# A graph layer's prologue done block by block: norm, projection and the first attention of a block in turn

## The chip, the cores and the metric

One core of one Trainium2 chip. The metric is the device time of one execution in microseconds (us). The kernel uses five engines that run side by side, each with its own instruction queue: TensorE (PE; its weight loads are listed as PEld), VectorE (DVE), ScalarE (ACT), GpSimd (POOL), and SyncE (SP), which here only issues DMAs. Matrix operands are 32-bit floats throughout.

## The reference

One layer of a graph transformer over 3125 nodes with 256 features and 100,000 edges. Its three branches are:

```python
xn = layernorm(x)                                           # no gain, no bias
# 1. graph branch
m   = relu(concat([xn[src], edge_attr], 1) @ W1.T + b1)     # 100000 x 256
h_N = segment_sum(m, dst)                                   # dst is sorted
g   = relu(concat([xn, h_N], 1) @ W2.T);  g = g / max(norm(g), 1e-12)
# 2. mixer: 4 layers of linear attention and a feed-forward part on xn
for i in range(4):
    h = layernorm(xm) * ln1_g[i] + ln1_b[i]
    q = softmax(heads(h @ Wq[i]) * s, over features)
    k = softmax(heads(h @ Wk[i]) * s, over nodes);  v = heads(h @ Wv[i])
    xm = xm + (q @ (k.T @ v)) @ Wo[i] + bo[i]
    h = layernorm(xm) * ln2_g[i] + ln2_b[i]
    xm = xm + gelu(h @ W1[i] + b1[i]) @ W2[i] + b2[i]
x = x + g + xm
# 3. mixture of experts: 16 experts, 2 for each node, then a layernorm
x = x + layernorm(y + moe(y)) * gamma + beta,  with y = layernorm(x)
```

The first step of mixer layer 0 is a layernorm of `xn`, which is itself a layernorm of `x`.

## The kernel before

The nodes lie in 25 tiles of 125 rows, grouped in seven blocks of 4, 4, 4, 4, 4, 3 and 2 tiles (`BLOCKS`). All 25 tiles stay on the chip in `xm`, which holds first `x`, then `xn`, then the mixer's running sum.

The prologue has four parts, written out one after the other. First, SP issues the loads: all of `x` in block order, then `w1h` (the node part of the graph branch's W1), `w1w` (its edge part), the bias `b1`, the edge indices `src_i` and `dst_i`, the norm gains `lnp`, and Wk, Wq, Wv of layer 0. Second, the destinations of the edges are turned into windows: `dst_i` is cast to `drel`, the least destination of each strip of edges is found (`least`, `lcol`, transposes `least_ps`, `base_ps` and `most_ps` on PE), and it is subtracted. Third, for each block: statistics (lines 90 and 91), a reciprocal root (`rsqrt`, lines 108 to 114, eleven small operations that depend on each other), a normalisation on DVE (line 122), transposes into `xnT` (line 144, copied out by ACT on line 244), and the projection `proj = xn @ w1h` (line 251), to which DVE adds `b1` (line 254) before it is stored to memory. Fourth, the attention of layer 0 is done block by block: statistics once more, a second `rsqrt` and normalisation into `xh1`, transposes `hT_ps` (stage_t1), k with a running maximum over nodes (stage_k), q (stage_q), transposes of exp(k) and q (stage_ek, stage_qT), and the sum over nodes `m_ps` (stage_m). When all blocks are summed, `context(l)` makes from it the matrix `mo` (first PE step `meanT_ps`), and the feed-forward part of layer 0 starts.

The edge work of the graph branch has no stage of its own. Edges come in 784 chunks of 128; eight chunks make one of 98 groups. `load_chunk` gathers the rows of `proj` for a chunk with an indirect DMA from POOL (line 273); `message_step` multiplies the edge features (`pw`, line 312), adds them to the gathered rows on DVE (line 316) and takes relu on ACT (line 317); `sum_step` sums a group into its windows on PE (`pq`, line 297), transposes (`win_ps`, line 288) and adds to `hNT` on DVE (line 291). A gather can start when all of `proj` is stored. These steps are dealt out between the mixer's matmuls: every stage calls `worked(columns)` with the columns that PE has just been given, the variable `place` advances by `columns * (98 + 1 + 1.25) / total`, and what is due by then is issued. `total` is the number of columns in four attentions and three feed-forward parts, so the edge work is spread from the first attention block to the end of mixer layer 2. Before a gather, POOL makes a one-element copy (`tick`, line 349) of something the stage has just written, so that gathers do not run ahead.

PE, ACT and POOL run in the order in which the program is written (`manual_schedule`); the order on DVE and SP is chosen by the framework's scheduler when the kernel is built.

Of the kernel before, what the change touches and what calls it, by code (L numbers as in the profile page):

```python
# [8 lines left out]
F32 = mybir.dt.float32  # L9
# [55 lines left out]
def gps_layer(ctx: ExitStack, tc: tile.TileContext, a, out):  # L65
# [60 lines left out]
    with ExitStack() as ph:  # L126
# [49 lines left out]
        b1 = tmp.tile([P, D], F32, tag="b2", name="b1")  # L176
# [6 lines left out]
        for r in BLOCKS:  # L183
            by_parts(nc.sync, xm[:, r[0]:r[-1] + 1, :], xv[:, r[0]:r[-1] + 1, :])
        nc.sync.dma_start(w1h, a["gnn_W1h"].rearrange("(c p) n -> p c n", p=P))
        for s in range(S):
            nc.sync.dma_start(w1w[s * W:s * W + 3, :], a["gnn_W1w"])
        nc.sync.dma_start(b1, rows_bcast(a["gnn_b1"], P))
        nc.sync.dma_start(src_i, a["src_c"])
        nc.sync.dma_start(dst_i, a["dst_c"])  # L190
        nc.sync.dma_start(lnp, a["mix_ln"])
        nc.sync.dma_start(ffb, a["mix_b1"])
        wt = {}

        def load(l, *names):
            for k in names:
# [4 lines left out]
        load(0, "Wk", "Wq", "Wv")  # L201


        nc.gpsimd.iota(slot, pattern=[[1, W]], base=0, channel_multiplier=0,
                       allow_small_or_imprecise_dtypes=True)
        nc.vector.tensor_copy(drel, dst_i)
        strips = drel.rearrange("p (g j) -> p g j", j=SC)
        least = edge.tile([P, NS], F32, name="least", bufs=1)
        nc.vector.tensor_reduce(least, strips, axis=AX.X, op=ALU.min)
        lcol = edge.tile([P, 1], F32, name="lcol", bufs=1)  # L210
        for s0 in range(0, NS, NG):
            part = least[:, s0:s0 + NG]
            ps = mm_tile("least_ps")[:NG, :P]
            nc.tensor.transpose(ps, part, ident)
            nc.vector.tensor_reduce(lcol[:NG], ps, axis=AX.X, op=ALU.min)
            ps = mm_tile("base_ps")[:, :NG]
            nc.tensor.transpose(ps, lcol[:NG].to_broadcast([NG, P]), ident[:NG, :NG])
            nc.vector.tensor_copy(part, ps)
        nc.vector.tensor_copy(base_i, least[:1, :])
        nc.vector.tensor_tensor(strips, strips, least[:, :, None].to_broadcast([P, NS, SC]),  # L220
                                op=ALU.subtract)

        for p0, p1 in ((NE % P, 2 * (NE % P)), (2 * (NE % P), P)):
            nc.vector.memset(drel[p0:p1, NCH - 1:NCH], -1.0)
        nc.vector.memset(drel[:, NCH:], -1.0)
        most = edge.tile([P, 1], F32, name="most", bufs=1)
        nc.vector.tensor_reduce(most, drel, axis=AX.X, op=ALU.max)
        ps = mm_tile("most_ps")[:1, :P]
        nc.tensor.transpose(ps, most, ident)
        nc.vector.tensor_reduce(most[:1], ps, axis=AX.X, op=ALU.max)  # L230
        nc.vector.tensor_scalar(far_i, most[:1], float(W), None, op0=ALU.is_ge)


        for r in BLOCKS:
            for t in r:
                stats(tmp, xm[:, t, :], t)
            finish_stats(r)
            for t in r:
                normalize(xm[:, t, :], xm[:, t, :], t)
            xnT = tmp.tile([P, KC, BT * TP], F32, tag="hT", name="xnT", bufs=2)  # L240
            for q in groups(len(r), 2):
                t0, n, o = r[q[0]], len(q), q[0] * TP
                ps = transposed(xm[:, t0:t0 + n, :], n, "xnT_ps")
                nc.scalar.copy(xnT[:, :, o:o + n * TP], ps)
            nc.sync.dma_start(xnT_d[:, :, cols(r[0], len(r))], xnT[:, :, :len(r) * TP])
            for q in groups(len(r), 2):
                t0, n, o = r[q[0]], len(q), q[0]
                pp = mm_tile("proj_ps")[:TP].rearrange("p (i d) -> p i d", d=D)
                for i in range(n):
                    for c in range(KC):  # L250
                        nc.tensor.matmul(pp[:, i, :], xnT[:, c, cols(o + i)], w1h[:, c, :],
                                         start=(c == 0), stop=(c == KC - 1))
                pj = tmp.tile([TP, 2, D], F32, tag="pj", name="pj", bufs=2)
                nc.vector.tensor_add(pj[:, :n, :], pp[:, :n, :],
                                     b1[:TP, None, :].to_broadcast([TP, n, D]))
                by_parts(nc.sync, by_tile(proj)[:, t0:t0 + n, :], pj[:, :n, :])
# [4 lines left out]
        def load_chunk(c):  # L261

            g, j = divmod(c, G)
            if j == 0:
                ea = edge.tile([P, SC * P], F32, name="ea")
                for s in range(S):
                    e0 = (g * S + s) * SC * P
                    nc.sync.dma_start(ea[s * W:s * W + 3, :], a["eaT"][:, e0:e0 + SC * P])
                groups_[g] = [], ea
            gats = groups_[g][0]  # L270
            if j % (G // 2) == 0:
                gats.append(edge.tile([P, 2, SC, D], F32, name="gat", bufs=6))
            nc.gpsimd.indirect_dma_start(  # L273
                out=gats[-1][:, (j // SC) % 2, j % SC, :], out_offset=None, in_=proj,
                in_offset=bass.IndirectOffsetOnAxis(ap=src_i[:, c:c + 1], axis=0))
# [26 lines left out]
        def message_step(g):  # L302
# [7 lines left out]
            for i in range(SC):  # L310
                for s in range(S):
                    nc.tensor.matmul(pws[s][:, i, :], ea[s * W:s * W + 3, i * P:(i + 1) * P],  # L312
                                     w1w[s * W:s * W + 3, :], start=True, stop=True)
# [23 lines left out]
        total = DEPTH * attention + (DEPTH - 1) * (forward + 60 * D)  # L337
        place = -LEAD
        tick = tmp.tile([1, 1], F32, name="tick")

        def worked(columns, mark=None):


            nonlocal place
            place += columns * (NG + 1 + LEAD) / total
# [17 lines left out]
        st = {}  # L363

# [249 lines left out]
        with tc.manual_schedule(engines=in_order):  # L614

            for b in range(NB + 1):
                if b < NB:
                    stage_stats(b)
                    stage_ln1(b)
                    stage_t1(0, b)  # L620
                if b > 0:
                    stage_ek(0, b - 1)
                    stage_qT(0, b - 1)
                if b < NB:
                    stage_k(0, b)
                    stage_q(0, b)
                if b > 0:
                    stage_m(0, b - 1)
            for l in range(last):
# [47 lines left out]
        def any_order():  # L677
# [13 lines left out]
            def chunk(e0, n):  # L691
# [15 lines left out]
                nc.sync.dma_start(ea[:3, :n], a["eaT"][:, ds])  # L707
# [17 lines left out]
                nc.tensor.matmul(pw[:n, 0, :], ea[:3, :n], w1w[:3], start=True, stop=True)  # L725
# [427 lines left out]
def device_arrays(inputs):  # L1153
# [14 lines left out]
    d = {"x": i["x"], "eaT": np.pad(i["edge_attr_3"].T, ((0, 0), (0, fill))), "src": i["src"], "dst": i["dst"]}  # L1168
    d["src_c"], d["dst_c"] = chunked(i["src"]), chunked(i["dst"])
    w1 = i["L0_gnn_W1"]  # L1170
    d["gnn_W1h"], d["gnn_W1w"] = w1[:, :D].T, w1[:, D:].T
    d["gnn_b1"] = i["L0_gnn_b1"]
# [33 lines left out]
```

## Time and profile before

| what | us |
|---|---|
| median of 3 runs (2003.48 to 2004.11) | 2003.74 |
| profiled execution, its own time | 1999.63 |
| its span, first to last instruction | 1997.9 |
| PE busy in the span | 1800.4 (90%) |
| DVE busy | 1188.0 (59%) |
| POOL busy | 1135.1 (57%) |
| ACT busy | 726.0 (36%) |
| mean granted TensorE clock | 0.958 of full |

The profiled execution is one run; its own time is 1.7 us over its span and 4.1 us (0.2%) under the median of the timed runs. The page divides the span into 40 slices of about 50 us. A group row gives line, engine, operation, names and shapes, count, then busy time and mean duration of one in ns, and after the second bar the idle time of that engine just before these instructions, with what ended it. A wait row names who waited for whom, the total in us, how often, and the longest. In the windows table each row is a stretch of the span, with the busy time of each engine in it. In the timeline, each row has a start, a length, the engine and line, what it writes and reads, and the idle time ahead of it in brackets.

### The profile page before, as it was taken

The numbers are of one execution on the slowest core, as the hardware profiler recorded it, in microseconds if no ns is written. First come the engines' busy times: TensorE is split into PE (matmuls) and PEld (weight loads), VectorE is DVE, ScalarE is ACT, GpSimd is POOL, SyncE is SP. The second block draws the span as 40 slices with busy tenths as digits, with TensorE's granted clock in tenths as the row PEclk, the third lists the DMA queues.
The fourth block names the chain that finished last, engine by engine and source line by source line (L and its number), as shares of the span: only waits on it lengthen the run. The fifth ranks groups of instructions, "written<-read, shape, count | busy, mean of one in ns | idle before, by whom it ended". The sixth has DMA issues, their size and how long they took to land. (4 is left out here: it accounts for less than half of the span.)

```text
span 1997.9 us, 30925 instructions
## 1 busy us (share of the span) xinstructions
PE 1800.4 (90%) x9749; PEld 1263.7 (63%) x9749; DVE 1188.0 (59%) x3910; ACT 726.0 (36%) x1305; POOL 1135.1 (57%) x1469
## 2 busy tenths in 40 slices
PE   2888899999988999999889999998999994999963
PEld 2656466666664666666646666676777783788841
DVE  8677546766666466767565667665555653333326
ACT  0344334434443444445433444453222221222212
POOL 1366766667666776767667776772213445555512
PEclk9998899999998999999989999998999996999977
DMA  6422322223243322323433222233211103777744
GB/s 186 139 78 84 103 77 76 83 75 89 83 134 89 91 83 76 89 78 92 128 94 90 79 86 78 86 86 114 66 32 27 30 19 97 251 260 261 267 131 127
DMA packets 83416, 210.46 MB, mean 105 GB/s; under 512 B 26287, under 2 KB 41927, under 8 KB 78510
## 3 DMA queue, kind: packets, MB, share of 16 engines
q0 software_dynamic: 44800, 118.16, 20.2%
q1 hardware_dynamic: 37368, 87.03, 13.8%
q10 hardware_dynamic: 1078, 3.20, 0.6%
q8 instruction: 83, 1.36, 0.3%
q14 instruction: 87, 0.71, 0.1%
HBM read 187.06 MB, written 21.19 MB: 104 GB/s over the span
## 5 line engine op out<-in xcount | busy, mean ns | idle before, releaser
L273 POOL DMA_INDIRECT gat<-proj,src_i x784 | 761.1, 971 | 219.1 <-issue 162.8
L542 PE MATMUL f_ps<-h2T,ww 128*128 128x500 f32 (+2 forms) x896 | 360.9, 551 | 8.3 <-ACT h2T L354 6.3
L317 ACT ACTIVATE gat<-gat 128x512 f32<-128x512 f32 x392 | 237.5, 630 | 343.3 <-DVE gat L316 322.6
L552 PE MATMUL f_ps<-ww,gT 128*125 128x256 f32 x1600 | 360.3, 381 | 0.0
L316 DVE TENSOR_TENSOR gat<-gat,pw 128x512 f32<-128x512 f32 x392 | 245.5, 680 | 154.6 <-PE pw L312 138.0
L552 PEld LDWEIGHTS f_ps<-ww,gT 128*125 128x125 f32 x1600 | 295.0, 188 | 55.5 <-issue 11.4
L542 PEld LDWEIGHTS f_ps<-h2T,ww 128*128 128x128 f32 x896 | 166.0, 192 | 172.6 <-issue 120.5
L544 ACT ACTIVATE gT<-f_ps,ffb 128x500 f32<-128x500 f32 (+2 forms) x224 | 135.4, 631 | 134.4 <-PE f_ps L542 133.7
L297 PE MATMUL pq<-gat,hot 128*32 128x256 f32 x1568 | 131.4, 402 | 11.2 <-ACT gat L317 10.8
L291 DVE TENSOR_TENSOR hNT<-hNT,win_ps 128x64 f32 x392 | 84.7, 216 | 69.1 <-PE win_ps L288 57.0
L866 POOL DMA_INDIRECT slots<-rec,at x50 | 59.5, 1189 | 110.3 <-DVE rs_u L113 64.1
L312 PE MATMUL pw<-w1w,ea 3*128 3x256 f32 x1568 | 116.2, 406 | 1.6 <-ACT ekT L408 1.6
L557 DVE TENSOR_TENSOR xm<-xm,f_ps 125x512 f32<-125x512 f32 (+1 forms) x52 | 34.7, 667 | 136.7 <-PE f_ps L552 133.9
L1061 PE MATMUL e_ps<-ew,hs 128*128 128x256 f32 x464 | 112.8, 381 | 2.2 <-DVE o L1065 2.2
L1068 POOL DMA_INDIRECT outs<-o,ids x58 | 57.4, 989 | 99.5 <-DVE o L1066 94.9
L508 PE MATMUL y_ps<-mo,qT 128*125 128x256 f32 x400 | 96.2, 391 | 6.7 <-DVE mo L499 6.7
L90 DVE BATCH_NORM_STATS2 bnst<-xm 125x6 f32<-125x256 f32 x250 | 97.9, 416 | 5.5 <-DMA xm<-x 3.4
L312 PEld LDWEIGHTS pw<-w1w,ea 3*128 3x128 f32 x1568 | 72.9, 187 | 44.1 <-issue 34.4
L456 PE MATMUL m_ps<-xh,ek 125*128 125x257 f32 x400 | 97.8, 397 | 1.3 <-ACT ek L442 1.3
L1061 PEld LDWEIGHTS e_ps<-ew,hs 128*128 128x128 f32 x464 | 85.2, 190 | 20.4 <-issue 4.5
L419 PE MATMUL q_ps<-wwq,hT 128*125 128x256 f32 x400 | 94.9, 387 | 3.6 <-DVE gat L316 2.4
L524 POOL TENSOR_TENSOR xm<-xm,b 125x1024 f32<-125x1024 f32 (+2 forms) x28 | 59.9, 2139 | 66.4 <-DVE xh L122 50.1
(210 smaller groups left out, 2631.7 us busy)
## 6 DMA issues: line engine op xcount, KB each, us to landing
ew<-ffn_w SPq DMA_DIRECT2D x37, 1154.0 KB
gat<-proj,src_i POOLq DMA_INDIRECT x784
ww<-mix_W SPq DMA_DIRECT2D x8, 1024.0 KB
ea<-eaT SPq DMA_DIRECT2D x392, 3.0 KB
proj<-pj SPq DMA_DIRECT2D x12, 224.0 KB
ogs<-outs SPq DMA_DIRECT2D x6, 448.0 KB
ogs<-outs ACTq DMA_DIRECT2D x6, 448.0 KB
out<-ogs SPq DMA_DIRECT2D x6, 448.0 KB
```

What stands on the lines that cost most here:

```text
L90: nc.vector.bn_stats(st, src)
L273: nc.gpsimd.indirect_dma_start(out=gats[-1][:, (j // SC) % 2, j % SC, :], out_offset=None, in_=proj, in_offset=bass.IndirectOffsetOnAxis(a ...
L297: nc.tensor.matmul(pq[s * W:(s + 1) * W, :], hot[:, s * SC + i, :], gats[s // 2][:, s % 2, i, :], start=(i == 0), stop=(i == SC - 1))
L312: nc.tensor.matmul(pws[s][:, i, :], ea[s * W:s * W + 3, i * P:(i + 1) * P], w1w[s * W:s * W + 3, :], start=True, stop=True)
L316: nc.vector.tensor_add(msg, msg, pws[s])
L317: nc.scalar.activation(msg, msg, AF.Relu)
L456: nc.tensor.matmul(ps, st["ek", b][:, i, c * P:(c + 1) * P], xh1s[b % 2][:, i, :], start=(i == 0), stop=(i == n - 1))
L508: nc.tensor.matmul(ps[:, i, :], qT[:, c, cols(t0 + i)], mo[:, c, :], start=(c == 0), stop=(c == KC - 1))
L542: nc.tensor.matmul(ps, wt["W1"][:, c, f * P:(f + 1) * P], st["h2T", b][:, c, :m], start=(c == 0), stop=(c == KC - 1))
L544: nc.scalar.activation(gT[:, f, :m], ps, AF.Gelu, bias=ffb[:, l, f:f + 1])
L552: nc.tensor.matmul(ps[:, i, :], st["gT", b][:, f, cols(o + i)], wt["W2"][:, f, :], start=(f == 0), stop=(f == NF - 1))
L1061: nc.tensor.matmul(ps[:, j, :], x["hs"][:, f, j * P:(j + 1) * P], x["w2"][:, f, :], start=(f == 0), stop=(f == NEF - 1))
```

## The change

The prologue's four parts become one loop over blocks. For a block, the norm, the projection and the attention follow each other, and the next block's norm and projection are written between the attention's stages of this one.

- The loads are put in the order of use: the first four tiles of `x` in two pairs, `w1h`, `lnp`, then the other blocks, with Wk and Wq after block 1 and `dst_i` after block 3; the rest comes last.
- The second layernorm's statistics are not taken. With v the variance of a row of `x` and e the small constant, a row of `xn` has mean 0 and variance v/(v+e), so the two norms follow from v: `stage_xn` computes v+e and (e(v+e)+v)(v+e), takes the reciprocal roots of both at once (`rs`, 8 columns for a block), normalises `xm` with the first, and multiplies to get the factor from `xn` to `xh1`. `stage_xh1` applies that factor on ACT.
- The bias `b1` becomes a fourth edge feature with value 1, so `eaT` and `w1w` have four rows in place of three, and the projection is copied out by ACT with no bias added. It is stored a block at a time. `xnT` and the projection are staged in the memory of `gT` and `xh`.
- The window computation becomes a generator, `windows()`, whose PE steps are issued one by one between the stages of blocks 2 to 5.
- `worked` does nothing until block 5 is through (`spread`), and `total` counts three attentions in place of four. So the edge work starts behind the sixth of seven blocks.

```diff
-        for r in BLOCKS:
-            by_parts(nc.sync, xm[:, r[0]:r[-1] + 1, :], xv[:, r[0]:r[-1] + 1, :])
-        nc.sync.dma_start(w1h, a["gnn_W1h"].rearrange("(c p) n -> p c n", p=P))
...
-        load(0, "Wk", "Wq", "Wv")
+        for r in (range(0, 2), range(2, 4)):
+            by_parts(nc.sync, xm[:, r[0]:r[-1] + 1, :], xv[:, r[0]:r[-1] + 1, :])
+        nc.sync.dma_start(w1h, a["gnn_W1h"].rearrange("(c p) n -> p c n", p=P))
+        nc.sync.dma_start(lnp, a["mix_ln"])
+        for i, r in enumerate(BLOCKS[1:]):
+            by_parts(nc.sync, xm[:, r[0]:r[-1] + 1, :], xv[:, r[0]:r[-1] + 1, :])
+            if i == 0:
+                load(0, "Wk", "Wq")
+            if i == 2:
+                nc.sync.dma_start(dst_i, a["dst_c"])
...
+        load(0, "Wv")
+        def windows():
...
+                yield
+                ps = mm_tile("least_ps")[:NG, :P]
+                nc.tensor.transpose(ps, part, ident)
...
-                pj = tmp.tile([TP, 2, D], F32, tag="pj", name="pj", bufs=2)
-                nc.vector.tensor_add(pj[:, :n, :], pp[:, :n, :],
-                                     b1[:TP, None, :].to_broadcast([TP, n, D]))
-                by_parts(nc.sync, by_tile(proj)[:, t0:t0 + n, :], pj[:, :n, :])
...
-                    nc.tensor.matmul(pws[s][:, i, :], ea[s * W:s * W + 3, i * P:(i + 1) * P],
-                                     w1w[s * W:s * W + 3, :], start=True, stop=True)
+                    nc.tensor.matmul(pws[s][:, i, :], ea[s * W:s * W + 4, i * P:(i + 1) * P],
+                                     w1w[s * W:s * W + 4, :], start=True, stop=True)
...
-        total = DEPTH * attention + (DEPTH - 1) * (forward + 60 * D)
+        total = (DEPTH - 1) * (attention + forward + 60 * D)
         place = -LEAD
+        spread = False
...
+            if not spread:
+                return
...
+        def stage_xn(b):
+            r = BLOCKS[b]
+            n = len(r)
+            for t in r:
+                stats(tmp, xm[:, t, :], t)
+            rs = tmp.tile([TP, 3, 2, BT], F32, name="rs", bufs=3)
...
+            nc.vector.tensor_scalar(rs[:, 0, 0, :n], v, EPS, None, op0=ALU.add)
+            nc.vector.scalar_tensor_tensor(rs[:, 0, 1, :n], rs[:, 0, 0, :n], EPS, v, op0=ALU.mult, op1=ALU.add)
+            nc.vector.tensor_mul(rs[:, 0, 1, :n], rs[:, 0, 1, :n], rs[:, 0, 0, :n])
+            rsqrt(rs[:, 1], rs[:, 0], rs[:, 2])
+            for i, t in enumerate(r):
+                nc.vector.tensor_scalar(xm[:, t, :], xm[:, t, :], mv[:, t, 0:1], rs[:, 1, 0, i:i + 1],
+                                        op0=ALU.subtract, op1=ALU.mult)
+            nc.vector.tensor_mul(rs[:, 2, 0, :], rs[:, 0, 0, :], rs[:, 1, 1, :])
+        def stage_xh1(b):
+            for i, t in enumerate(BLOCKS[b]):
+                nc.scalar.activation(xh1s[b % 2][:, i, :D], xm[:, t, :], AF.Copy,
+                                     scale=st["rs", b][:, 2, 0, i:i + 1])
+        def stage_xnT(b):
...
+                ps = transposed(xm[:, t0:t0 + n, :], n, "xnT_ps")
+                nc.scalar.copy(xnT[:, :, cols(o, n)], ps)
+            nc.sync.dma_start(xnT_d[:, :, cols(r[0], len(r))], xnT[:, :, :len(r) * TP])
+        def stage_proj(b):
...
+                        nc.tensor.matmul(pp[:, i, :], st["xnT", b][:, c, cols(o + i)], w1h[:, c, :],
+                                         start=(c == 0), stop=(c == KC - 1))
+                nc.scalar.copy(pj[:, o:o + n, :], pp[:, :n, :])
+            by_parts(nc.sync, by_tile(proj)[:, r[0]:r[-1] + 1, :], pj[:, :len(r), :])
...
+            prepared = windows()
+            stage_xn(0)
+            stage_xh1(0)
+            stage_xnT(0)
+            stage_proj(0)
+            stage_xn(1)
+            stage_t1(0, 0)
             for b in range(NB + 1):
                 if b < NB:
-                    stage_stats(b)
-                    stage_ln1(b)
-                    stage_t1(0, b)
-                if b > 0:
-                    stage_ek(0, b - 1)
-                    stage_qT(0, b - 1)
-                if b < NB:
                     stage_k(0, b)
+                    if b + 2 < NB:
+                        stage_xn(b + 2)
                     stage_q(0, b)
+                if b > 1:
+                    next(prepared, None)
                 if b > 0:
                     stage_m(0, b - 1)
+                if b + 1 < NB:
+                    stage_xh1(b + 1)
+                    stage_xnT(b + 1)
+                    if b > 1:
+                        next(prepared, None)
+                    stage_proj(b + 1)
+                    stage_t1(0, b + 1)
+                if b < NB:
+                    if b > 1:
+                        next(prepared, None)
+                    stage_ek(0, b)
+                    stage_qT(0, b)
+                if b == NB - 2:
+                    for _ in prepared:
+                        pass
+                    spread = True
```

## The prediction

> **What bounds the kernel now.** I read the page first, then the start of the span in the windows table, then PE's waits, the timeline of PE, and POOL's groups.
>
> ```profile
> span 1997.9 us, 30925 instructions
> PE 1800.4 (90%) x9749; PEld 1263.7 (63%) x9749; DVE 1188.0 (59%) x3910; ACT 726.0 (36%) x1305; POOL 1135.1 (57%) x1469
> ...
> 0.00:38.00 38.00, 2.92 (x9) 1.29 (x10) 32.88 (x192) 1.28 (x1) 6.12 (x8) 1.00 0.70 194
> 38.00:70.80 32.80, 30.50 (x151) 25.50 (x151) 24.31 (x127) 6.79 (x13) 0.00 (x0) 1.00 0.53 179
> 70.80:200.50 129.70, 110.85 (x677) 78.82 (x676) 89.87 (x233) 57.03 (x112) 79.39 (x122) 0.95 0.30 85
> 200.50:240.00 39.50, 32.08 (x170) 18.04 (x171) 23.41 (x82) 12.96 (x22) 27.88 (x34) 0.83 0.35 103
> 240.00:600.00 360.00, 347.98 (x2023) 234.47 (x2021) 227.48 (x671) 159.10 (x282) 247.59 (x352) 0.98 0.30 88
> ```
>
> PE bounds the middle (348 of 360 us busy from 240 to 600), so time is to be had where PE idles. In the first 38 us PE works 2.9 us; DVE is busy for 32.9.
>
> ```profile
> PE least_ps L214 <- DVE rs_u L113: 30.4, 1, 30.4
> ```
>
> PE's queue begins with the window transposes, whose input DVE makes after most of its norms: 30.4 us in one wait, the largest of PE.
>
> ```profile
> 38.02 1.87 PE L144 MATMUL xnT_ps<-ident,xm 125*128 125x125 f32 x8
> 39.73 4.76 PE L251 MATMUL proj_ps<-w1h,xnT 128*125 128x256 f32 x16
> 44.32 1.02 PE L144 MATMUL xnT_ps<-ident,xm 125*128 125x125 f32 x8
> 45.58 3.72 PE L251 MATMUL proj_ps<-w1h,xnT 128*125 128x256 f32 x16 [0.24 <-ACT xnT L244]
> 49.13 1.02 PE L144 MATMUL xnT_ps<-ident,xm 125*128 125x125 f32 x8
> ...
> 222.35 1.82 PE L144 MATMUL h2T_ps<-ident,xh 125*128 125x125 f32 x8 [3.85 <-DVE xh L122]
> 224.10 2.09 PE L312 MATMUL pw<-w1w,ea 3*128 3x256 f32 x16
> 226.12 0.69 PE L288 MATMUL win_ps<-ident,osb 128*128 128x128 f32 x2
> ```
>
> The prologue then runs densely, at a fixed price for a block. After an idle stretch the same instructions cost nearly double.
>
> ```profile
> L273 POOL DMA_INDIRECT gat<-proj,src_i x784 | 761.1, 971 | 219.1 <-issue 162.8
> L297 PE MATMUL pq<-gat,hot 128*32 128x256 f32 x1568 | 131.4, 402 | 11.2 <-ACT gat L317 10.8
> L312 PE MATMUL pw<-w1w,ea 3*128 3x256 f32 x1568 | 116.2, 406 | 1.6 <-ACT ekT L408 1.6
> ```
>
> POOL needs 0.97 us for a gather and mostly 0.30 us more to issue it; PE loses only 10.8 us to messages not ready.
>
> **The change, part by part.** I mark the end of the prologue by meanT, the first PE step after the last sum over nodes. Before, it starts at 200.5.
>
> *The new prologue.* By starts in the timeline a full block takes PE: xnT 0.9, proj 3.55 (45.58 to 49.13), hT 0.9, k 3.45, q 3.5, exp(k) 0.9, qT 0.85, m 3.65, together 17.7 us. For 6.25 blocks that is 110 us; window transposes, short blocks and meanT make it 114. To this come PE's idle times. I walked PE, ACT and DVE through their orders in the built program with durations from the groups:
> - First transposes at 9.4. Two tiles of x land near 4 (before, four landed at 5.2); four statistics with their aggregates 2.0, fourteen dependent small operations at 0.19 from start to start 2.7, two normalisations 0.7.
> - proj(0) 1 us later (ACT applies xh1's factor to four tiles, about 0.4 each, before it copies xnT).
> - k(0) waits 5: in DVE's queue its hT stands behind the statistics and small operations of blocks 2 and 3, the cast of dst_i (0.55) and `least` (0.97).
> - proj(1) waits 4: ACT's queue has q's exponentials, four xh1, then xnT.
> - The next five blocks wait 1.2 each, 6 together; the last qT and meanT 3.6 (short block, nothing between).
> That is 29 idle. The clock after the three long gaps: below.
>
> DVE is no bound here: per block 4 statistics and aggregates 1.9, fourteen small operations 2.7, normalisations 1.4, halves of hT 0.9, k 1.7, q 5.2, m 0.8, together 14.6 under 19 us. What leaves DVE (25 statistics of 0.416, 25 normalisations of 0.406, seven rsqrt, 13 bias adds of about 0.69) was on the path before 38 us and in DVE's way later; its worth is in the walk, not added. ACT gains 25 scalings (0.416, the row of exp on 125x256) and 13 copies (0.585, the row of 125x512): about 10.5 us a block, under PE's.
>
> *The clock.* After the 3.85 us gap at 222.35, transposes, pw and win took 1.82, 2.09 and 0.69 us where 1.02, 1.15 and 0.38 are usual: 2.05 lost up to there. [...] by the row, with 2.3 each, 7 and a sum of 150. I take the row. With 2 us for semaphores and DMA order (0 to 5), meanT starts at 152, 48.5 earlier.
>
> *The edge work is put off, not saved.* By 200.5 the kernel before has done eight pw (about 1.1 each), eight pq (1.07, one 1.57), seven win (0.32 to 0.5): 19.4 us of PE. That moves behind meanT: +19.4. It stays inside layers 0 to 2, so nothing after them changes.
>
> *Denser gathers.* A group came every 636,680/100.25 = 6351 columns, now every 579,330/100.25 = 5779. From 240 to 600, 216 gathers (27 groups) took a group per 13.3 us; 572 columns fewer at 1.76 ns (3.6 us per 2048) make 12.3. POOL's need there: gathers 209.7 and 59.7 idle before them, adds 15, ticks 25.6: 310/27 = 11.5 us, so 93% in place of 86%. It holds on average. At a layer's start five calls stand for 15,360 columns that PE does not spend: 19 gathers before, 21 now. POOL was already late there (0.8 and 1.8 us of waits for messages at 227 to 232), so two gathers of 1.25 more cost up to 2.5, three times: +6 (0 to 9). The first layer also starts with no lead: gathers begin about 140 (proj(6) copied out at 138, stored 2 us later) and eight need 10.4 us, so the first message is ready near 153, when PE asks. DVE holds ctxT and `mo` behind that wait: +3 (0 to 6) for this and other jitter.
>
> *Costed at nothing.* Four feature rows in place of three: pw with 3 rows takes 406 ns, y with 128 rows 391, so rows are free; ea DMAs of 4 KB for 3 KB land a group ahead. `rs` on 8 columns for 4: nearest row 149 ns at 4, bounds 0 to 0.03 each, off the path after block 0. The reordered loads on SP: xnT_d, proj and Wo now stand in SP's queue behind each other's ACT waits, but each is used 15 us or more after its issue; only proj(6) is followed at once, by the gathers, and is in the sum. If x's blocks landed 1 to 2 us later, all shifts by as much (within the 0 to 5).
>
> **Sum.** -48.5 + 19.4 + 6 + 3 = -20.1 against the profiled execution's 1999.63, so 1979.5. The median is 4.1 above the profiled run; I add that back: 1983.6, say 1984.
>
> **The rivals.**
> - A, larger gain. Denser edge work fills gaps (PE idles 12 us from 240 to 600), and layer starts cost nothing: -48.5 + 19.4 = -29, with 3 from filling -32: 1972. For: pw and pq need no fresh result of the mixer. Against: POOL is late at layer starts already.
> - B, slower: POOL becomes the bound in layers 0 to 2. PE then waits for gathers in every group. Its need is 11.5 of 12.3 us; the gain of 29 is used up when a group of 98 loses 0.30 us, that is from a need of 12.6, a gather pitch of 1.39 in place of 1.25 (269.4/216). With 0.40 lost it is 39 us: 2014. For: POOL cannot run ahead (ticks), and its adds of 2.4 us sit in the same queue. Against: the last chunk of a group is issued 0.75 of a group (9 us) before its use; DMA moves only about 85 GB/s here.
> - C, the prologue stalls at every block. DVE and ACT are in order; if each of seven blocks waits 3 us more and falls to the slow clock (2 us), meanT comes 35 later, of which 15 are already counted: 20 lost, so 2004, or 1998 where layer 0's gathers, then ready, give part of it back. For: k(0) and proj(1) show such waits. Against: from block 2 on, norms are written two blocks ahead.
> That the edge work might shrink is excluded: same 784 gathers and matmuls.
>
> **How the numbers follow.** Main case 0.50 (its own range 1976 to 1992), A 0.24 (1966 to 1976), C 0.15 (1992 to 2006), B 0.11 (2000 to 2020). The range 1968 to 2000 holds the main case, most of A and more than half of C: about 0.8. A measurement of this kernel can tell about 0.2%, 4 us. Faster by more: 0.50 + 0.24 + 0.11 of C = 0.85. Same (1999.7 to 2007.7): 0.05. Slower: 0.10.
>
> **What would show it.** Right: no wait for least_ps; PE's first transposes at 9 to 11 us; blocks 2 to 5 at 19 to 20 us each; meanT at 150 to 156; first gather near 140; PE's wait for relu'd messages at 15 to 20 us in place of 10.8; from the end of layer 2 on, all groups as before. Wrong: meanT after 165 (C), gathers without pause from 240 to 1340 and PE's waits for messages over 40 us (B), or first transposes after 14 us.

## The result, and the profile after

| what | before | after |
|---|---|---|
| median, us (6 runs each) | 2003.70 (2000.19 to 2004.34) | 1989.60 (1985.53 to 1994.73) |
| profiled execution, its own time | 1999.63 | 1994.73 |
| its span | 1997.9 | 1993.0 |
| first meanT | 200.52 | 140.72 |
| first to fourth meanT (layers 0 to 2) | 1201.35 | 1254.10 |
| after the fourth meanT | 596.13 | 598.18 |

The ratio is 0.9931, with an interval of 0.9915 to 0.9947: 0.7% faster. The profiled execution after is the slowest of its six, so its gain (5 us) is smaller than the medians' (14 us). All lines below are of the profiled executions.

The page of the changed kernel shows nearly the same work: PE is busy 7 us longer than before, DVE 23 less, ACT 18 more:

```profile
span 1993.0 us, 30766 instructions
PE 1807.7 (91%) x9749; PEld 1269.3 (64%) x9749; DVE 1165.1 (58%) x3761; ACT 743.6 (37%) x1343; POOL 1126.5 (57%) x1429
...
L255 POOL DMA_INDIRECT gat<-proj,src_i x784 | 761.9, 972 | 212.4 <-issue 163.4
L279 PE MATMUL pq<-gat,hot 128*32 128x256 f32 x1568 | 137.6, 405 | 22.4 <-ACT gat L299 22.3
L294 PE MATMUL pw<-w1w,ea 4*128 4x256 f32 x1568 | 114.6, 403 | 0.0
```

PE has as many matmuls as before, the fourth feature row costs nothing (403 ns where three rows took 406), and PE's wait for relu'd messages has doubled, from 10.8 to 22.3 us.

The windows table, cut at the first and the fourth meanT, tells where the time went. Columns: length, then busy time of PE, PEld, DVE, ACT and POOL, the granted clock, the DMA share. Before:

```profile
0.00:200.52 200.52, 144.27 (x835) 105.64 (x836) 147.08 (x551) 65.13 (x126) 85.53 (x130) 0.97 0.41 121
200.52:1401.87 1201.35, 1142.77 (x6666) 762.57 (x6667) 755.22 (x2285) 517.33 (x913) 817.29 (x1146) 0.97 0.31 90
1401.87:1998.00 596.13, 513.31 (x2249) 395.53 (x2247) 285.70 (x1075) 143.53 (x267) 232.24 (x194) 0.93 0.41 130
```

After:

```profile
0.00:140.72 140.72, 117.46 (x566) 92.62 (x566) 96.67 (x338) 59.76 (x124) 12.07 (x18) 0.98 0.36 109
140.72:1394.82 1254.10, 1176.72 (x6936) 780.60 (x6937) 782.11 (x2349) 540.07 (x952) 882.27 (x1218) 0.96 0.33 93
1394.82:1993.00 598.18, 513.54 (x2249) 396.10 (x2247) 286.30 (x1075) 143.75 (x267) 232.21 (x194) 0.93 0.41 131
```

The prologue is 59.8 us shorter, the three layers are 52.75 us longer, and the rest is 2 us longer. Of the layers' 52.75, PE's busy time is 33.95 (270 matmuls of edge work came over, which the prediction priced at 19.4; at that price the other 14.5 are matmuls taking longer) and PE's idle time is 18.8.

PE's timeline of the new prologue, one block after another (in brackets: idle time before, and what ended it; the load of Wq in the first row is no input of these transposes, whose `xm` DVE normalises from 9.46 us on):

```profile
9.98 2.00 PE L144 MATMUL xnT_ps<-ident,xm 125*128 125x125 f32 x8 [9.98 <-DMA wwq<-mix_Wq]
13.16 5.69 PE L399 MATMUL proj_ps<-w1h,stage 128*125 128x256 f32 x16 [1.19 <-ACT stage L389]
18.69 1.02 PE L144 MATMUL hT_ps<-ident,xh 125*128 125x125 f32 x8
20.44 1.11 PE L432 MATMUL k_ps<-hT,wwk 128*128 128x500 f32 x2 [0.73 <-ACT hT L339]
24.02 4.46 PE L432 MATMUL k_ps<-hT,wwk 128*128 128x500 f32 x6 [2.47 <-DVE hT L341]
...
36.70 5.40 PE L399 MATMUL proj_ps<-w1h,stage 128*125 128x256 f32 x16 [3.91 <-ACT stage L389]
...
44.52 3.52 PE L432 MATMUL k_ps<-hT,wwk 128*128 128x500 f32 x8
...
56.19 3.72 PE L399 MATMUL proj_ps<-w1h,stage 128*125 128x256 f32 x16 [0.36 <-ACT stage L389]
...
140.72 0.80 PE L521 MATMUL meanT_ps<-ident,mean 128*128 128x128 f32 x4 [1.37 <-DVE mean L516]
```

The wait of 30.4 us for least_ps is gone. Two waits of the first blocks remain, k(0) for DVE (2.47 us) and proj(1) for ACT (3.91); from block 2 on PE hardly waits.

### The profile page after: what moved, and what is told of

The parts are those of the page before. It is cut to its first block, busy times and chain, and to the rows that moved or that the text cites. A ratio compares the mean times of both kernels' runs of the same rounds, so it can differ in the third digit from the quotient of the medians.

```text
span 1993.0 us, 30766 instructions
## 1 busy us (share of the span) xinstructions
PE 1807.7 (91%) x9749; PEld 1269.3 (64%) x9749; DVE 1165.1 (58%) x3761; ACT 743.6 (37%) x1343; POOL 1126.5 (57%) x1429
## 2 busy tenths in 40 slices
DMA packets 83294, 210.74 MB, mean 106 GB/s; under 512 B 26523, under 2 KB 42306, under 8 KB 78389
## 3 DMA queue, kind: packets, MB, share of 16 engines
q0 software_dynamic: 44800, 118.16, 20.6%
## 5 line engine op out<-in xcount | busy, mean ns | idle before, releaser
L279 PE MATMUL pq<-gat,hot 128*32 128x256 f32 x1568 | 137.6, 405 | 22.4 <-ACT gat L299 22.3
L294 PE MATMUL pw<-w1w,ea 4*128 4x256 f32 x1568 | 114.6, 403 | 0.0
L458 PE MATMUL q_ps<-wwq,hT 128*125 128x256 f32 x400 | 99.8, 402 | 4.6 <-DVE gat L298 3.6
L294 PEld LDWEIGHTS pw<-w1w,ea 4*128 4x128 f32 x1568 | 72.5, 185 | 45.0 <-issue 34.5
L279 PEld LDWEIGHTS pq<-gat,hot 128*32 128x32 f32 x1568 | 49.6, 112 | 77.9 <-ACT gat L299 45.3
```

Of the source, the lines that this page charges most:

```text
L279: nc.tensor.matmul(pq[s * W:(s + 1) * W, :], hot[:, s * SC + i, :], gats[s // 2][:, s % 2, i, :], start=(i == 0), stop=(i == SC - 1))
L294: nc.tensor.matmul(pws[s][:, i, :], ea[s * W:s * W + 4, i * P:(i + 1) * P], w1w[s * W:s * W + 4, :], start=True, stop=True)
L458: nc.tensor.matmul(ps[:, i, :], hT[:, c, cols(o + i)], wt["Wq"][:, c, :], start=(c == 0), stop=(c == KC - 1))
```

## The experiments

They ran on other chips than the first comparison, and there the kernel before takes 2177 (one execution) to 2193 us in place of 2003. A ratio here is always to the kernel before on the same chip; three of these chips agree on its median to 0.1% (2190.45, 2191.80, 2192.87), so ratios from different chips are set beside each other with some 0.3% in hand, not less.

I called the theory that gathers come late where the edge work is dense P, and the theory that DVE's additions of messages stand ahead of the mixer's work in DVE's queue D. Both try to explain the 33 us that the layers lost beyond the moved work.

### The two kernels on the slower chips: c_before, c_after

> The kernel before itself, for one look at where its time lies on a chip on which it takes 2190 us in place of 2003. The stretch after the last meanT has taken 596 to 598 us in every kernel on every chip, so 187 us more must lie ahead of it. Theory (the chips differ only where gathers run beside the rest): the first 160 us as on the first chip, the last part of the prologue some 5 to 10 longer (first meanT at 205 to 211), and layers 0 to 2 near 1385 (1201 on the first chip). Then the changed kernel's 1489 us there is a loss of some 104, of which 19 are moved work. Rival (the chip is slower throughout): the first meanT at 215 or later, or a last stretch over 610.

> The changed kernel itself, as the control for the three beside it. In the first comparison it was 0.9931 of the kernel before, with the prologue 59.8 us shorter and layers 0 to 2 52.7 us longer. If the layers' loss is a matter of the order of instructions alone, the same two numbers come again (ratio 0.991 to 0.995, meanT at 140 to 141, layers 0 to 2 near 1254 us). If it is a matter of how fast the chip serves the many transfers in flight, the ratio may be another on another chip (0.98 to 1.02) while meanT stays at 140 to 141.

The kernel before took 2182.81 us in its one execution, the changed kernel 2223.20 (2216.76 to 2230.59; ratio 1.0139, 1.0120 to 1.0159): **here the change makes it slower.** The layers of the kernel before in the windows table, then the changed kernel's prologue and layers on another of these chips:

```profile
209.79:1584.84 1375.05, 1229.17 (x6667) 798.35 (x6667) 761.57 (x2285) 520.87 (x913) 816.49 (x1146) 0.93 0.27 78
```

```profile
0.00:142.17 142.17, 118.58 (x566) 93.48 (x566) 96.70 (x338) 59.77 (x124) 12.06 (x18) 0.96 0.37 108
142.17:1631.18 1489.01, 1283.46 (x6936) 826.36 (x6937) 786.77 (x2349) 542.35 (x952) 878.50 (x1218) 0.90 0.28 79
```

The new prologue is as short as on the first chip (142.2), and the stretch after the last meanT takes the same 597 us. What differs is the part in which gathers run beside the mixer: the kernel before needs 1375 us for it in place of 1201, the changed kernel 1489 in place of 1254. So the loss in the layers is 114 us here, of which 19.4 are moved work, if it costs what it did on the first chip, against a gain of 67.6 in the prologue. These two executions lie further apart than the kernels do: their spans differ by 47.7 us, the medians on one chip by 31.4, so some 16 of the 114 belong to the two executions and chips. PE's idle time there is 145.9 us before and 205.6 after, and the rest is the moved work and a lower clock (0.93 and 0.90). The expectation's theory held: the chips differ only where gathers run beside the rest, the end of the old prologue among it (first meanT at 209.8, 205 to 211 said).

### The late edge work alone: e1_late_edges

```diff
-        total = DEPTH * attention + (DEPTH - 1) * (forward + 60 * D)
+        total = (DEPTH - 1) * (attention + forward + 60 * D)
+        spread = False
...
+            if not spread:
+                return
...
+                if b == NB - 1:
+                    spread = True
```

> The kernel before with one part of the change alone: the edge work starts with the k stage of the last block and total counts three attentions; the prologue keeps its four parts. Theory (the loss is made by spreading the edge work over fewer columns): the three layers, meanT of layer 0 to meanT of layer 3, take 1245 to 1258 us as in the changed kernel (1254.1) and not 1201.4 as before; meanT of layer 0 comes 25 to 35 us earlier than 200.5, since 19.4 us of edge work and the stalls around it leave the prologue; the whole is 15 to 28 us slower than before. Rival (the changed kernel lost its gain by something else in its new prologue, such as late gathers at its end only): the layers take 1201.4 + 19.4 + 2 = about 1223 us, and the whole is within 10 us of before.

Measured: 2264.06 us (ratio 1.0330, 1.0307 to 1.0354), 73.6 us slower than the kernel before, where 15 to 28 was expected from the first chip's numbers. Its windows:

```profile
0.00:181.12 181.12, 124.14 (x565) 96.83 (x565) 122.03 (x487) 44.71 (x86) 12.06 (x18) 0.96 0.28 85
181.12:1664.66 1483.54, 1285.91 (x6936) 826.57 (x6937) 793.32 (x2349) 542.61 (x952) 880.58 (x1218) 0.90 0.27 79
```

The layers take 1483.5 us, as in the changed kernel (1489.0), although nothing else of the change is in; the rival, under which the layers gain only the moved work and 2 us, would give about 1397 (1375 and 22). So on these chips all of the layers' loss comes from the edge work being put off and packed closer; the fourth feature row, the new prologue and the order of loads have no part in it that shows. The prologue without edge work is 181.1, which is 28.7 us under the 209.8 of the kernel before on this kind of chip (25 to 35 expected): the edge work and the stalls around it.

### Density: e5_sparse

```diff
-        total = (DEPTH - 1) * (attention + forward + 60 * D)
+        total = 1.099 * (DEPTH - 1) * (attention + forward + 60 * D)
```

> The changed kernel with a group of edges every 6351 columns of PE as before, instead of every 5779; about nine groups are then left over and run in one piece after layer 2, bound by POOL at some 10 us a group, so the whole is about 50 to 75 us slower than the changed kernel and says nothing by itself. What counts is the stretch from the first to the third meanT (layers 0 and 1; 842.5 us in the first profile of the changed kernel, 805.9 before). Fewer groups there take 14 us of PE's work away. Theory P or D (the density of the edge work costs the 33 us): about 805 to 815. Rival (the density does not matter; what matters is that the first gathers start without lead, or the bursts at layer starts): about 828, the 14 us alone.

The stretch from the first to the third meanT (layers 0 and 1) of the kernel before, of the changed kernel and of this one:

```profile
209.79:1141.30 931.51, 825.98 (x4467) 532.62 (x4467) 509.97 (x1529) 350.12 (x613) 558.03 (x779) 0.92 0.27 78
```

```profile
142.17:1141.48 999.31, 858.22 (x4668) 549.11 (x4669) 528.57 (x1575) 367.62 (x642) 606.71 (x837) 0.90 0.28 80
```

```profile
141.33:1074.27 932.94, 821.69 (x4446) 534.12 (x4447) 505.03 (x1513) 347.60 (x608) 556.66 (x778) 0.91 0.27 78
1074.27:1632.60 558.33, 458.58 (x2491) 288.72 (x2491) 283.47 (x837) 196.07 (x344) 324.61 (x444) 0.86 0.28 80
```

With a group every 6351 columns again, layers 0 and 1 take 932.9 us: the 931.5 of the kernel before, and 66.4 less than with a group every 5779, of which fewer groups explain 14. The lead is missing here too, and the bursts stand where they stood, a tenth smaller; the two starts, from meanT to the first f1 (the first matmul of the feed-forward part), gave 12.3 of the 66.4 (83.6 us against 95.9). So the density decides, mostly between the starts, and the missing lead does not. Against the expectation the whole is no slower than the changed kernel (2224.57 against 2223.20): the nine groups left over and run in one piece cost 68.6 us in the last line (558.3 against 489.7), no more than spread out. On these chips a group squeezed in between costs as much as one that stands alone.

### What the bursts and the lead are worth: e6_start7, e3_lead2, e2_no_tick

e6 counts a credit of 12\*256 columns at a layer's start as 7\*256; e3 has `LEAD = 2.0` in place of 1.25; e2 drops the copies by which POOL paces its gathers:

```diff
-                    nc.gpsimd.tensor_copy(tick, mark)
+                    pass
```

> The changed kernel with the five credits at each layer start cut from 12*256 to 7*256 columns, so that 1.5 groups instead of 2.7 are asked for in a burst there; the total is cut with it, so a group comes every 5587 columns elsewhere. Theory P (POOL is late where a burst meets it): the stretch from meanT to the first f1 falls from 38/31/31 us by 6 to 9 each, of which the moved pw and pq are 3; the whole is 8 to 15 us faster than the changed kernel. Theory D (DVE's adds stand ahead of the mixer's work everywhere): the starts only give back what the denser rest takes, so within 5 us of the changed kernel, or up to 8 slower.

> The changed kernel with a lead of 2.0 groups in place of 1.25 for the gathers, messages and sums as they were, so a chunk's gather is issued 1.5 groups ahead of its use in place of 0.75. Density rises by 0.75 of 100 groups (0.7%). Theory P: the wait of pq for messages falls from 22.3 to under 8 us and the whole gains 8 to 15 us. Theory D: gain of 0 to 6 us. Where edge work starts 0.75 of a group later after the prologue, up to 2 us of it are given back.

> The changed kernel without the one-element copies on POOL ahead of gathers, so that gathers run ahead as far as their six buffers allow. Theory P (POOL's lateness with gathers is what the layers lost): PE's wait of pq for relu'd messages falls from 22.3 us to under 6, the layers take 15 us less than 1254, the whole 10 to 20 us less than the changed kernel. Theory D (the additions of messages on DVE stand ahead of the mixer's own work, whatever POOL does): that wait falls, but the waits of qT (22.8 us) and h2T (14.6 us) stay, and the whole gains 0 to 8 us. A third outcome is slower: gathers that run ahead take DMA or POOL time from the bias additions on POOL, and h2T or f1 wait for them.

| kernel | us | ratio to before | layers 0 to 2, us |
|---|---|---|---|
| c_after | 2223.20 | 1.0139 | 1489.0 |
| e6_start7 | 2209.39 | 1.0086 (1.0061 to 1.0112) | 1469.1 |
| e3_lead2 | 2208.58 | 1.0083 (1.0063 to 1.0102) | 1465.4 |
| e2_no_tick | 2367.16 | 1.0813 (1.0785 to 1.0842) | 1626.4 |

e6: the three stretches from meanT to the first f1 fall from 48.9, 47.0 and 45.1 us to 37.2, 32.3 and 35.8, together by 35.7; P had said 6 to 9 for each. The layers as a whole gain 19.9 by it, so 16 come back in the denser rest. The whole gains 14, which is in P's 8 to 15, with about half of what the starts gave. e3 gains some 12, also in P's range; PE's waits for messages fall from 57 us (39.2 for ACT, 17.9 under "issue", where the profile names nothing) to 35, not under the 8 that P said.

e2 speaks against P as the whole story. Its expectation had named "slower" as a third outcome. Without the copies POOL runs ahead as far as buffers let it: by the traces a gather starts 31 us (median) before DVE adds to its rows, 15 in the changed kernel, and a run of gathers that start under 1.4 us apart is 7 long on average in place of 4. PE's waits in its layers:

```profile
PE f_ps L591 <- issue: 44.8, 56, 1.7
PE pw L294 <- issue: 34.3, 29, 3.6
PE pq L279 <- issue: 28.5, 28, 5.6
PE pq L279 <- ACT gat L299: 27.0, 18, 4.0
PE f_ps L581 <- issue: 26.8, 7, 19.5
PE qT_ps L144 <- DVE qs L469: 26.6, 5, 9.2
```

In front of pq PE stands no longer than in the changed kernel (27.0 and 28.5 us; there 39.2 for ACT and 17.9 under "issue"), and yet the layers are 137 us longer: PE's idle time is 96 us more, over half of it now under "issue" (161 of 298 us of waits, 40 of 205 in the changed kernel), and its matmuls take 42 us more at a granted clock of 0.86. DVE and ACT are not busy longer (784.5 and 541.5 us; 786.8 and 542.4 in the changed kernel), so the time goes to pauses, not to slower instructions. So on these chips taking the pacing away holds up the other work although the gathers are early. That the bunching does it is the reading I hold; the trace does not show what the pauses wait for.

### POOL's other work: e4_b2_dve, e8_before_b2_dve

The changed kernel and the kernel before, each with the second bias added by DVE:

```diff
-            nc.gpsimd.tensor_add(xs, xs, b2[:TP, None, :].to_broadcast([TP, len(r), D]))
+            nc.vector.tensor_add(xs, xs, b2[:TP, None, :].to_broadcast([TP, len(r), D]))
```

> The changed kernel with the addition of b2 (28 operations of 2.1 us on POOL, 21 of them in layers 0 to 2) moved to DVE, where it takes about 1.2 us each by the row of 125x512 (0.67 to 0.69 us). Theory P (a gather stands behind an addition that waits for DVE, 7.2 us once at 163 to 170): POOL has 60 us less to do, pq's wait falls by 8 us or more, the whole gains 5 to 12 us. Theory D: DVE gets 33 us more in order ahead of the mixer's work, and the whole loses 3 to 15 us.

> The kernel before with one edit: the addition of the second bias to x after the second norm is made by DVE instead of POOL (28 additions of 2.1 us). The same edit made the changed kernel faster. Theory P (POOL's gathers are late only where the edges come as densely as in the changed kernel): POOL had slack before, so the gain is small, 0 to 8 us, and the edit cures what the change brought. Rival (POOL's additions cost the layers the same at any density): a gain of 25 to 45 us on a chip where the kernel before takes 2190 us, or 10 to 20 where it takes 2003.

The additions of layers 0 to 2 in the groups of the changed kernel, and of e4:

```profile
L563 POOL TENSOR_TENSOR xm<-xm,b 125x1024 f32<-125x1024 f32 (+2 forms) x21 | 45.1, 2149 | 39.5 <-DVE xh L122 19.8 <-issue 11.5 <-DVE hNT L273 7.9
```

```profile
L563 DVE TENSOR_TENSOR xm<-xm,b 125x1024 f32<-125x1024 f32 (+2 forms) x21 | 23.3, 1110 | 0.9
```

DVE does one in half the time and hardly waits for it; on POOL 45.1 us of work have 39.5 us of idle time in front of them, in which the gathers behind stand still. DVE's additions of messages take 0.682 us on average in the layers of the changed kernel, where POOL adds beside them, and 0.681 in e4, where it does not, so no slowing of DVE by POOL's addition shows; the queue on POOL remains. e4 takes 2176.33 us (ratio 0.9930, 0.9910 to 0.9950) where the changed kernel has 1.0139: about 2.1%, or 46 us, where P said 5 to 12. e8 takes 2163.60 (0.9863, 0.9842 to 0.9885), 29 us under the kernel before. D as the main cause falls on these chips: DVE was given 23 us more, and PE got faster. P in its narrow form (late only at the new density) falls too, since POOL's additions cost a good deal at the old density, as e8's rival said. At the new one they cost half as much again, with some 7 us of doubt on each figure.

### Parts of the prologue: e7_windows_first, e10_own_norm

e7 runs the window generator dry at once and loads `dst_i` early; e10 takes the known variance back:

```diff
             prepared = windows()
+            for _ in prepared:
+                pass
```

```diff
-            for i, t in enumerate(BLOCKS[b]):
-                nc.scalar.activation(xh1s[b % 2][:, i, :D], xm[:, t, :], AF.Copy,
-                                     scale=st["rs", b][:, 2, 0, i:i + 1])
+            stage_stats(b)
+            stage_ln1(b)
```

> The changed kernel with all window transposes at the head of PE's queue again and dst_i loaded early, as before; the blocks in turn, the known variance and the bias as an edge feature stay. If the head of the queue was what held PE for its first 38 us only because DVE did 25 norms in front of it, meanT comes 8 to 12 us later than in the changed kernel (a cast of 0.55, the minimum of 0.97, four round trips PE to DVE of about 1.5, the rest) and the whole is 8 to 12 us longer. Rival: the window transposes were themselves most of the gain: meanT 25 us later or more.

> The changed kernel with the known variance taken back: the mixer's first norm computes its own statistics of the normalised x, its reciprocal root and its normalisation on DVE, as before, where the changed kernel has ACT scale the normalised x by one factor per row. All else stays. DVE gets 1.9 us of statistics, 2.5 of small operations and 1.6 of normalisation more in each block, which brings it from 14.6 to 20.6 us in a block of 18: DVE bounds the prologue, and block 0 has 6 us more on the path. meanT comes 15 to 25 us later than in the changed kernel (140.7). Rival (ACT's scalings cost as much as they save, since xnT's copies stand behind them in ACT's queue): meanT within 5 us.

e7: 2232.01 us (1.0194, 1.0164 to 1.0225). PE's head of the queue:

```profile
10.21 0.42 PE L218 MATMUL least_ps<-ident,least 128*98 128x128 f32 x1 [10.21 <-DVE rs L112]
15.54 0.42 PE L222 MATMUL base_ps<-ident,lcol 98*128 98x98 f32 x1 [4.92 <-DVE lcol L219]
...
22.50 0.37 PE L235 MATMUL most_ps<-ident,most 128*1 128x128 f32 x1 [3.46 <-DVE most L232]
22.67 1.87 PE L144 MATMUL xnT_ps<-ident,xm 125*128 125x125 f32 x8
```

PE comes to xnT at 22.7 instead of 10, waits less for k(0) afterwards, and meanT is at 150.9: 8.7 us after c_after's, as expected. So of the 67.6 us on these chips, 28.7 are edge work and its stalls that left (209.8 to 181.1), 8.7 the moved window transposes, and 30.2 the rest of the new prologue (181.1 to 150.9). That rest is the work in blocks, by which DVE's norms run beside PE's matmuls, the bias as an edge feature and the order of loads; no run took these three apart.

e10: 2220.81 us (1.0127, 1.0104 to 1.0150), meanT at 138.5, no later than in the eight other traces with this prologue (138.8 to 142.2). **The known variance brings nothing.** Two blocks of e10, then two of the changed kernel on the first chip:

```profile
45.87:63.56 17.69, 17.45 (x89) 13.94 (x88) 17.54 (x74) 7.70 (x15) 0.00 (x0) 1.00 0.48 167
63.56:81.20 17.64, 17.51 (x91) 14.16 (x90) 17.59 (x94) 7.78 (x15) 0.00 (x0) 1.00 0.17 59
```

```profile
56.19:74.00 17.81, 17.56 (x90) 14.02 (x90) 12.32 (x39) 9.17 (x20) 0.00 (x0) 1.00 0.17 59
74.00:91.80 17.80, 17.75 (x91) 14.19 (x91) 12.29 (x40) 9.13 (x20) 0.00 (x0) 1.00 0.17 58
```

DVE's busy time goes from 12.3 us a block to 17.5 beside PE's 17.5: just full, and PE is not held up. My 20.6 came from the prediction's 14.6 for a block, where 12.3 are measured: it counts small operations from start to start as if nothing ran in their pauses.

### Three edits at once: e9_three

The changed kernel with e4's, e6's and e3's edits.

> The changed kernel with three edits at once, each of which helped alone: the second bias added by DVE, the credits at a layer's start cut to 7*256 columns, and gathers issued up to 2 groups ahead instead of 1.25. If all three act on one thing (gathers that come late), they add up in part: 0.983 to 0.992 of the kernel before where it takes 2190 us, and 0.972 to 0.982 where it takes 2003 (prologue -59.8, moved edge work +19.4, and little of the 33 us left). If they act on different things they add up fully: 0.980 to 0.983, or under 0.972.

Measured: 2167.92 us (0.9882, 0.9842 to 0.9922), layers 1434.6 us (e4 alone 1445.7). Four fifths of it is e4; the other two add 0.5% where alone they gave 0.5% each. In full they would have given 0.982, just under the interval, so they seem to act on one thing in part; with 0.3% in hand between chips this is not shown. e9 and e8 beat both kernels on these chips, and cannot be told apart. On the first chip's kind neither was run.

## Why the prediction was right, and where it wasn't

It said 1984 us, and the median is 1989.6: inside the range and inside the main case. The nearness is in part luck. Two terms were mis-sized in opposite directions, the prologue by 11 us and the layers by 24. Between the profiled executions, on which the sum was built, the gain is 4.9 us where 20.1 was said; the medians lie closer because the changed kernel's profiled execution is its slowest. And on the other chips the forecast would have had the wrong sign. The mechanism, a shorter prologue paid for in part by denser gathers, held.

**The prologue: -48.5 said, -59.8 found.** The sum was 121 us of PE's work with the slow clock, and 31 of idle time and slack; measured are 117.5 busy and 23.3 idle. Step by step: the first transposes 9.98 (9.4 said), proj(0) 1.19 (1), k(0) 0.73 + 2.47 (5), proj(1) 3.91 (4), the later blocks 1.8 together (6), the last qT and meanT 3.2 (3.6). meanT at 140.7 lies outside the 150 to 156 that was named as a sign of being right. The step that failed is "the next five blocks wait 1.2 each": they wait 0.2 to 0.7, and a block takes 17.8 us, not 19 to 20. The 2 us of slack, an allowance for which no row was shown, were not needed either. The start and the stall of proj(1) came as walked, k(0)'s two waits were 3.2 in place of 5.

**The clock.** Against their later twins, xnT (2.00 for 1.02), proj(0) (5.69 for 3.72), the six k of block 0 (4.46 for 2.64, by 3.52 for eight) and proj(1) (5.40 for 3.72) lost 6.4 us. The prediction took 7 by the row: 2.3 for each of three gaps (the start, k(0), proj(1)), an estimate from the one gap of 3.85 us in the kernel before; it was 0.6 too high. k(0) lost 1.8 us after an idle time of 2.47 us, with two matmuls and another 0.73 in front of it, so a gap shorter than that row's slowed PE too; proj(1) lost 1.7 after 3.91. The granted clock was 1.00 from 20 to 24 us and 0.62 from 24 to 28.5.

**The moved edge work: +19.4.** PE's busy time in the prologue is 144.27 in the kernel before and 124.14 in e1, which has the old prologue without edge work: 20.1 less, on another chip. The price was right to about 1 us; the pieces that the prediction lists for it add up to 20 to 21. (That 200.5 less 181.1 is 19.4 as well is chance: it sets one chip's meanT against another's.)

**The denser gathers: +9 said, 33 found (52.75 less 19.4).** The starts of layers, from meanT to the first f1, were not the failure: 38.5, 31.0 and 31.4 us after, 33.0, 30.9 and 22.8 before, so 14.3 more with about 2 of moved work in it, where 9 was said. The step that failed is "It holds on average", which put the layers between the starts at nothing: there they became 38.5 us longer. Of this some 17 is moved work, 11.0 is idle time of PE (43.3 before, 54.3 after), and 10 is matmuls that took longer. PE's and DVE's waits in the layers, after:

```profile
PE qT_ps L144 <- DVE qs L469: 22.8, 7, 4.9
PE pq L279 <- ACT gat L299: 22.3, 16, 3.9
DVE gat L298 <- DMA gat<-proj,src_i: 20.5, 11, 4.1
...
PE h2T_ps L144 <- DVE gat L298: 7.1, 4, 1.9
```

Before:

```profile
PE qT_ps L144 <- DVE qs L430: 16.1, 6, 4.1
...
DVE gat L316 <- DMA gat<-proj,src_i: 13.8, 6, 4.1
...
PE pq L297 <- ACT gat L317: 10.8, 10, 1.9
...
PE h2T_ps L144 <- DVE gat L316: 1.6, 1, 1.6
```

The row of gathers that come late, pq, is near what was said (15 to 20 said, 22.3 found), but most of its growth is in the starts (4.3 to 12.8 us); between them it is 6.5 before and 9.5 after. What grew there are the waits for DVE, which the sum did not have: qT by 6.7 us and h2T (the transposes behind a layer's second norm) by 5.5. They are not late gathers: no wait of DVE for a gather stands within 20 us ahead of any of them. DVE is at work, and in the two longest of qT it has four additions of messages ahead of q's softmax, as theory D says (before, in one of six). One of them:

```profile
536.03 2.47 DVE L298 TENSOR_TENSOR gat<-gat,pw 128x512 f32<-128x512 f32 x4
538.42 0.69 DVE L464 TENSOR_REDUCE qm<-q_ps 125x16 f32<-125x512 f32 x1
```

```profile
542.57 0.82 PE L144 MATMUL qT_ps<-ident,qs 125*128 125x125 f32 x4 [4.89 <-DVE qs L469]
```

A late gather, on POOL and then on PE, in the start of the changed kernel's layer 0:

```profile
170.55 2.36 POOL L563 TENSOR_TENSOR xm<-xm,b 125x1024 f32<-125x1024 f32 x1 [7.22 <-DVE hNT L273]
...
173.19 0.99 POOL L255 DMA_INDIRECT gat<-proj,src_i  x1 [0.16 <-PE pq L279]
```

```profile
177.46 1.80 PE L279 MATMUL pq<-gat,hot 128*32 128x256 f32 x10 [3.86 <-ACT gat L299]
```

POOL waits 7.22 us in order to add a bias, the next gather starts only behind that, at 173.19, and PE stands 3.86 us for the message and then runs slow (1.80 us for ten matmuls, where 16 usually take 1.07). The 14.5 us of matmuls that took longer were not in the sum at all. The granted clock of the layers fell from 0.97 to 0.96; an estimate from these rounded figures, 0.03 of 1201 us against 0.04 of 1254, gives 14 us more lost to the clock, which is the size. So, by this estimate, waits cost clock as well. How the idle time splits between late gathers and additions that stand ahead on DVE stays open on this chip: no experiment ran on its kind.

**The rivals.** A (larger gain because the denser work fills gaps) and C (a stall in every block) did not happen. B has the right place and on the first chip the wrong size. Its figure, a loss of more than 29 us that uses up the gain, came true on the slower chips, but not by its mechanism: POOL is busy there for 878.5 of 1489.0 us and stands idle for 285 ahead of its pacing copies (85 on the first chip), and in e2 gathers issued earlier made it worse.

## What to carry to other kernels

Work that is put off is paid for again where it lands (here 19.4 us of it came with 52.75 us in the layers): price the stages that receive it with their own idle rows, not by a mean rate that still fits under 100%. In the queue of the engine that issues gathers, other work that has to wait was costly here (29 and 46 us for 28 additions), but the copies that pace the gathers also wait, and without them this kernel is some 6.5% slower on the slower chips: try each before taking it out. And a step that saved instructions on an engine off the path (the known variance, 5.2 us of DVE a block) was worth nothing here, since DVE had the room: with them it was busy 17.5 us of a block of 17.7 and PE was not held up.

## What was not expected of the hardware

- The sign of this change depends on the chip: 0.9931 on one, 1.0139 on another, with the new prologue and the last stretch the same within 2 us. Only where gathers of edges run do they differ (layers 0 to 2 of the kernel before: 1201 against 1375 us). Of the faster kind one chip was measured.
- Half of the landings are missing from a trace of the slower chips. The trace of the changed kernel holds 20,445 landings of transfers on the first chip and 10,379 on the second, for the same 784 gathers and, to one, the same DMA packets (83,294 and 83,293); from 600 to 700 us a gather shows 16 landings on average in the one and 5 in the other. "remote" and part of "issue" in those traces may stand where the releasing event is not there. Busy times do not rest on those events (DVE in the layers 782.1 us on the first chip and 786.8 on the second), but the causes read above from the wait rows of these chips (e2, e3, e4) are weaker. What makes these chips pause while gathers run was not shown.
- PE's clock fell through short gaps. At the first layer's start of the changed kernel, four gaps of 0.33, 1.34, 1.23 and 0.78 us between 144 and 153 us stood ahead of y, which took 5.61 us there and 3.72 for its next half; the granted clock was 0.66 from 144 to 153 and 0.50 from 153 to 157.
